# The first part of layer 3 for the last image moved into the loop of the attention layer, with the last chunk convolved in two turns

## The chip, the cores and the metric

The kernel runs on one core of a Trainium2 chip. A core has five engines with queues of their own: TensorE (PE, matrix products), VectorE (DVE), ScalarE (ACT), GpSimd (POOL) and SyncE (SP), which here only issues DMA transfers. An engine takes its instructions in order and waits on semaphores for what others must have finished. On-chip memory is SBUF (128 partitions) and PSUM, into which TensorE writes; DRAM is reached through DMA queues. The metric is the device time of one execution in microseconds. Three runs of the kernel before took 3888.66, 3891.05 and 3893.82 us: the median is 3891.05.

## The reference

A batch of four images of 64 x 64 pixels with 128 channels goes through four layers, one after the other. Layer 0 is neighbourhood attention, layer 1 full attention over the 4096 pixels of an image, layer 2 a gated product with a sum over a row and a layer norm. The change is about layer 3, a selective scan in four directions:

```python
xz = x @ Win                                   # 128 -> 2 x 256
xb, z = jnp.split(xz, 2, axis=-1)
xb = depthwise_conv3x3(xb)                     # 256 channels
xb = jax.nn.silu(xb + conv_b)                  # "u"
xf = xb.reshape(Bb, Cd, L); xt = transposed(xb).reshape(Bb, Cd, L)
xs = jnp.stack([xf, xf[..., ::-1], xt, xt[..., ::-1]], axis=1)
xs_flat = xs.reshape(Bb * K, Cd, L)
x_dbl = jnp.einsum('bcl,cd->bdl', xs_flat, Wxproj)
dt, Bs, Cs = x_dbl[:, :r], x_dbl[:, r:r + N], x_dbl[:, r + N:]     # r = 8, N = 1
dt_kb = dt.reshape(K, Bb, r, L)                # the reshape mixes batch and direction
u_kb = xs_flat.reshape(K, Bb, Cd, L)           # delta, B and C likewise
# scan over L: h = exp(softplus(dt @ Wdt + b) * A) * h + delta * u * B;  y = h * C + u * D
y = (y0 + y1 + y2 + y3).transpose(0, 2, 1)     # directions turned back
yz = y * jax.nn.silu(z)
out = layer_norm(yz) @ Wout
```

The reshape `(Bb * K)` to `(K, Bb)` gives "direction" k of the scan the four stacked sequences of image k, so each image must be through the first part of layer 3 (projection, convolution, SiLU, x_dbl) before its quarter of the scan can run.

## The kernel before, in words

`conv_seq` calls `layers_0_to_2` (L109) and then `layer_3` (L919). Every image is cut into 8 chunks of 512 pixels (8 rows).

**`layers_0_to_2`** runs the images one after the other. For image b it runs layer 0, then `layer_1` (L504 to L624), a loop over 34 steps i. A step scores one block of 128 queries against all keys (L581), copies the scores to SBUF (L584), folds a maximum on VectorE (L586 to L593), subtracts and exponentiates (L598 to L608), multiplies by v (L614) and finishes the block (reciprocal L618, residual L619). At the end of each step the loop calls `between(i)`, which lays other work beside the attention:

- one of four parts of layer 2 for chunk n, at i = 6 + 4n + part: mix (o at L671 on VectorE and L672 on POOL), py (L683), norm (L685 to L700), transpose (L248, L704) and a store of the result x to x3_d (x_d in the profile);
- one step of layer 3's first part, the closure `turn(i)` that `front(b)` (L720 to L883) returns.

After the loop `between` is called for four more i, with layer 0 of the next image taken two pieces at a time between them.

**`front(b)`** works on eight chunks during the attention of image b: chunks 4 to 7 of image b-1, then 0 to 3 of image b, each taking four steps, r = 0 to 3. Steps: `load` xc from x3_d; `project` (two matmuls pi into the tile xh, whose rows are shared with the next chunk); `gate` (two matmuls pz at L758, Silu to zf, store); `begin` (the middle tap on ScalarE), `multiply` (four taps as ScalarE products gsum and tp at L785 and L789, which `add_parts` sums on POOL at L796 and L799) and `add_taps` (four taps on VectorE, L805). `activate` (Silu into the one buffer u0, L808) comes at i = 4k + 7 for the k-th chunk, the last one at i = 33; `lower` (L815 to L832) a step later makes du = D*u, the product pd with Wxproj and its copy dq, stores them in du_d and dbl_d, and loads the row of B, spread over 128 partitions, as bb; `times_b` two steps after activate multiplies u by bb on POOL (L837) and stores it in ub_d. Silus are kept in program order on ScalarE; most of the rest the framework's scheduler may place.

Image 3 has no next image. Its chunks 4 to 7 are done at the start of **`layer_3`**, in a block of its own (L1001 to L1130) with other code: it loads weights (mb, cw, cc, pick), loads the tiles x3T of chunks 3 to 7, makes the output weights gw and bw, projects on PE (L1040, L1045), convolves with three taps on PE (L1057) and six on VectorE (L1064), makes u, du, pd (L1080), a product that spreads B over the partitions (pb, L1092) and multiplies on VectorE (L1105). In the same block zs and zt, the sums of D*u over the images in both orders (2 MB each, for f = 0 and 1), are loaded, added on POOL (L1112, with du at L1074) and stored in z_d; C of images 0 to 2 is transposed (`turn_c`, L969 to L971: load 16 KB, one transpose, a copy, store).

**The scan** (L1132 to L1232) has 64 steps, each for a pair of sequences and 1024 elements: pdt (L1169), Softplus de (L1177), inp = de * ub on POOL (L1179), Exp h (L1189), scan on VectorE (L1203), product with C on VectorE (L1219, or L1214 into yo, added to y by an accumulating DMA on POOL's queue, L1215). For the sequences of image k and direction b with b>>1 equal to k>>1, z_d is added to y by such a DMA as well (L1221). ub and cb are double-buffered tiles of 2 MB (ub_0 and ub_1, cb_0 and cb_1), loaded by SP a part ahead. `turn_c` of image 3 comes after step 1. An output stage follows.

Of the kernel before, what the change touches and what calls it, by code (L numbers as in the profile page):

```python
# [29 lines left out]
P = 128  # L30
# [46 lines left out]
def conv_seq(ctx, tc, x, mata, matb, cols, rows, rpb, dtw, convw, sel, out):  # L77
# [12 lines left out]

    ub_d, zf_d = stored("ub_d"), stored("zf_d")
    du_d = [[dram.tile([P, L], F32, name=f"du_d{i}_{f}") for f in range(2)] for i in range(2)]
    dbl_d = [dram.tile([NDBL, L], F32, name=f"dbl_d{b}") for b in range(B)]
    fronts = x3_d, ub_d, zf_d, du_d, dbl_d
# [9 lines left out]

    layers_0_to_2(tc, xf, mata, matb, rows, rpb, convw, ident, cl, dram, *fronts)
    layer_3(tc, of, matb, dtw, convw, sel, ident, cl, dram, *fronts)


@with_exitstack  # L109
def layers_0_to_2(ctx, tc, xf, mata, matb, rows, rpb, convw, ident, cl, dram, x3_d, ub_d, zf_d, du_d, dbl_d):  # L110
# [605 lines left out]

    def by_image_rows(t):
        return t.rearrange("p (i j) -> p i j", j=W)

    def front(b):  # L720
# [3 lines left out]
        u = wp.tile([P, 2, CH], F32, name="u0", tag="bm1")  # L724
        x_of, parts_of, sums = {}, [], {}
# [5 lines left out]
        def project(i, n):  # L731
# [5 lines left out]
            if n == 4:  # L737
                nc.gpsimd.tensor_copy(xh[:, me, :, 0, :], kept_row)
            elif n > 0:
                nc.gpsimd.tensor_copy(xh[:, me, :, 0, :], xh[:, 1 - me, :, RC, :])  # L740
                nc.gpsimd.tensor_copy(xh[:, 1 - me, :, RC + 1, :], xh[:, me, :, 1, :])
# [11 lines left out]

        def gate(i, n):
            x = x_of.pop((i, n))
            for f in range(2):
# [4 lines left out]
                tc.keep_in_program_order(nc.scalar.activation(zf, pz, AF.Silu))  # L761
# [12 lines left out]
        def taps(n):  # L774

            v = (1, 0) if n < NCH - 1 else (-1, 0)
            return [v, (-1, 1), (1, -1), (1, 1)], [(-v[0], 0), (0, -1), (0, 1), (-1, -1)]

        def multiply(n, f, which):
            for k in which:  # L780
                dy, dx = taps(n)[0][k]
# [4 lines left out]
                else:  # L786
# [3 lines left out]
                    parts_of.append((n, f, k, p))  # L790

        def add_parts():
            for n, f, k, p in parts_of:
                r0, r1, c0, c1 = region(n, *taps(n)[0][k])
                a = by_image_rows(sums[n, f])[:, r0:r1, c0:c1]
                nc.gpsimd.tensor_tensor(a, a, p, ALU.add)  # L796
                if k == 3:
                    acc = accs[n & 1][:, f, :]
                    nc.gpsimd.tensor_tensor(acc, acc, sums.pop((n, f)), ALU.add)  # L799
            parts_of.clear()  # L800

        def add_taps(n, f):
            for dy, dx in taps(n)[1]:
# [3 lines left out]
        def activate(n):  # L807
            tc.keep_in_program_order(nc.scalar.activation(u, accs[n & 1], AF.Silu))  # L808

        def lower(i, n):  # L810

            lo, hi = CH * n, CH * n + CH
            for f in range(2):
                du = tmp.tile([P, CH], F32, name="du", tag="c512", bufs=9)
                nc.scalar.activation(du[:, ::-1] if i & 1 else du, u[:, f, :], AF.Copy, scale=cl("d", 2 * i + f))  # L815
# [5 lines left out]
            for f in range(2):  # L821
                for g in range(4):
                    nc.tensor.matmul(
                        pd[HD * g:HD * g + HD, :], lhsT=wx[:, f, :], rhs=u[:, f, bass.ts(g, P)],
# [4 lines left out]
            for g in range(4):  # L829
                nc.sync.dma_start(dbl_d[i][:, lo + P * g:lo + P * g + P], dq[HD * g:HD * g + NDBL, :])  # L830
            bb = x_of[i, n, "b"] = tmp.tile([P, CH], F32, name="bb0", tag="c512", bufs=9)
            nc.sync.dma_start(bb, dbl_d[i][RANK:RANK + 1, lo:hi][0].partition_broadcast(P))  # L832

        def times_b(i, n):
            bb = x_of.pop((i, n, "b"))
            for f in range(2):
                nc.gpsimd.tensor_tensor(u[:, f, :], u[:, f, :], bb, ALU.mult)  # L837
                nc.sync.dma_start(ub_d[i][f][:, bass.ts(n, CH)], u[:, f, :])
# [5 lines left out]
        takes += [[(b, j)] for j in range(4)] + [[]]  # L844

        def turn(i):
# [8 lines left out]
            if j < 8:  # L855
                if r == 0:
                    for c in takes[j]:
                        project(*c)
                    if j == 7:
                        project_row(b, 4)  # L860
                if now:
                    if r in (0, 2):
                        begin(now[1], r // 2)
                    multiply(now[1], r // 2, ((0, 1), (2, 3))[r & 1])
                    if r in (1, 3):
                        add_taps(now[1], r // 2)
# [6 lines left out]
            for k, c in enumerate(whole):  # L873
                at = 4 * k + 7 if k < 7 else 33
                if c:
                    if i == at:
                        activate(c[1])
                    if i == at + 1:
                        lower(*c)
                    if i == at + 2:  # L880
                        times_b(*c)
# [7 lines left out]
    for b in range(B):  # L889
# [25 lines left out]
        for i in range(NT + 2, NT + 6):  # L915
# [7 lines left out]
def layer_3(ctx, tc, of, matb, dtw, convw, sel, ident, cl, dram, x3_d, ub_d, zf_d, du_d, dbl_d):  # L923
    nc = tc.nc
    def pool(name, bufs=1, **kw):
# [11 lines left out]
    bc_d = [  # L937
        [dbl_d[b][RANK:RANK + 1, :], dbl_d[b][RANK + 1:RANK + 2, :], dram.tile([1, L], F32, name=f"ct_d{b}")]
        for b in range(B)
    ]  # L940

    mb = wp.tile([P, NMB], F32, name="mb")
    nc.sync.dma_start(mb, matb)
    win, wout, wx = (MB[k][0] for k in ("win", "wout", "wx"))

    dbl = wp.tile([P, L], F32, name="dbl")
    done = CH * 4
# [6 lines left out]


# [3 lines left out]
    nc.vector.memset(eps, 1e-5)  # L959
    def by_rows(t):  # L960
        return t.rearrange("p (i j) -> p i j", j=W)

    pick = wp.tile([P, 2, P], F32, name="pick")
    nc.sync.dma_start(pick, sel)

    cts = [wp.tile([W, 2, W], F32, name="ct")] * B

    def turn_c(b, pt):
        nc.tensor.transpose(pt, cts[b][:, 0, :], ident[0:W, 0:W])  # L969
        nc.scalar.copy(cts[b][:, 1, :], pt)  # L970
        nc.sync.dma_start(by_rows(bc_d[b][2])[0], cts[b][:, 1, :])  # L971
# [23 lines left out]

    taps_pe = [(0, 0), (0, -1), (0, 1)]
    taps_ve = [(-1, 0), (-1, -1), (-1, 1), (1, 0), (1, -1), (1, 1)]
    with pool("u", 8) as up, pool("z") as zp, pool("a", 2) as ap, pool("psB", 2, space=PSUM) as psp:  # L1000


        zs = [zp.tile([P, L], F32, name=f"zs{f}") for f in range(2)]
        cw = ap.tile([P, 3, DI], F32, name="cw", tag="cw", bufs=1)
        nc.sync.dma_start(cw, convw[3:6].partition_broadcast(P))
        nc.vector.tensor_tensor(cw, cw, mb[:, win:win + DI].unsqueeze(1).to_broadcast([P, 3, DI]), ALU.mult)
        cc = ap.tile([P, 2, 9], F32, name="cc", tag="cc", bufs=1)
        for f in range(2):
            nc.scalar.dma_start(cc[:, f, :], convw[:, P * f:P * f + P].rearrange("t p -> p t"))
        x3s = {}  # L1010
        for n in range(3, NCH):
            x3s[n] = ap.tile([P, RC, W], F32, name="x3T", tag="x3T", bufs=NCH - 3)
            nc.sync.dma_start(x3s[n], by_rows(x3_d[B - 1][:, bass.ts(n, CH)]))
        for f in range(2):
            nc.vector.tensor_scalar(
                gw[:, f, :], mb[:, wout + C * f:wout + C * f + C], cl("gamma", f), None, ALU.mult
            )
        pb = psp.tile([P, C], F32, name="pb", tag="d")
        for f in range(2):
            bb = ap.tile([P, P], F32, name="bb", tag="bb", bufs=1)  # L1020
            nc.vector.tensor_copy(bb, cl("beta", f).to_broadcast([P, P]))
            nc.tensor.matmul(pb, lhsT=bb, rhs=mb[:, wout + C * f:wout + C * f + C], start=(f == 0), stop=(f == 1))
        nc.vector.tensor_copy(bw, pb)
        share = ap.tile([P, P], F32, name="share", tag="bb", bufs=1)
        nc.vector.memset(share, 1.0 / DI)
# [423 lines left out]
```

## Time and profile before

| quantity | value |
|---|---|
| time of the profiled execution | 3889.84 us |
| its span in the profile | 3888.1 us |
| median of three runs | 3891.05 us |
| PE busy | 3405.7 us (88%) |
| DVE busy | 2775.9 us (71%) |
| ACT busy | 2692.5 us (69%) |
| POOL busy | 1438.4 us (37%) |
| last L618 of images 0, 1, 2, 3 starts at | 780.88, 1555.92, 2336.46, 3114.44 us |
| first pdt of the scan (L1169) starts at | 3227.86 us |

The span is the time from the first to the last record of the profile; some 1.7 us of the execution lie outside it. The profile cuts the span into 40 slices and gives for each the busy share of the engines in tenths. Windows give the same for any stretch, in us. The chain of waits goes back from the last instruction to what released it, again and again: each of its rows has a start, a length, an engine, and a tile or a line. A duration of an instruction is that of its line in the profile. DMA shares are the mean of 16 engines.

### The profile page before, as it was taken

How to read it: one execution, taken by the hardware profiler on the slowest of the kernel's cores; microseconds unless marked ns; L12 is line 12 of the kernel's file. 1: busy time of each engine (PE TensorE's matmuls, PEld its weight loads, DVE VectorE, ACT ScalarE, POOL GpSimd, SP SyncE). 2: the span in 40 equal slices, each digit the busy share in tenths (PEclk: the TensorE clock that was granted, in tenths of full speed). 3: DMA queues.
4: the chain of work that ended last, by engine and by line, in shares of the span. 5: the costliest groups of instructions: out<-in, count | busy, mean ns of one | idle time of the engine just before them, and what ended most of it. 6: DMA issues, size and time to landing. Idle time of an engine off the chain costs nothing.

```text
span 3888.1 us, 68949 instructions
## 1 busy us (share of the span) xinstructions
PE 3405.7 (88%) x26660; PEld 2788.6 (72%) x26660; DVE 2775.9 (71%) x4854; ACT 2692.5 (69%) x4364; POOL 1438.4 (37%) x1535
## 2 busy tenths in 40 slices
PE   6999999989999999899999998999999956665647
PEld 3679999956799998567999995679999822222236
DVE  3657777746677877467778774667787746998978
ACT  3865676767677766686777676767776737998944
POOL 5500022144122222451222214512222245897866
PEclk8999999999999999899999998999999975555569
DMA  5100000131010112310111012100011166998998
GB/s 138 46 1 27 12 13 29 48 95 34 17 48 31 37 31 50 92 35 17 47 28 40 31 48 95 34 17 26 28 37 34 29 228 188 278 272 255 260 280 288
DMA packets 192529, 325.07 MB, mean 84 GB/s; under 512 B 24257, under 2 KB 112190, under 8 KB 185246
## 3 DMA queue, kind: packets, MB, share of 16 engines
q1 hardware_dynamic: 150568, 251.75, 18.6%
q0 software_dynamic: 18624, 58.07, 8.1%
q10 hardware_dynamic: 23008, 10.84, 1.0%
q8 instruction: 210, 3.44, 0.4%
q14 instruction: 119, 0.97, 0.1%
HBM read 179.00 MB, written 108.11 MB: 74 GB/s over the span
## 4 chain that ended last, share of the span: by engine, by line
PE 52%; DVE 18%; ACT 12%; issue 7%; DMA 6%; POOL 4%; SPq 1%; POOLq 0%; ACTq 0%; DVEq 0%
PE po L614 16%; PE sc L581 16%; DVE mx L593 4%; PE pt L465 3%; DVE mx L588 2%; POOL inp L1179 2%; PE sc L430 2%; PE po L476 2%; DMA y<-yo 2%; ACT pr L448 2%; ACT st L584 2%; DVE h L1203 2%; ACT st L608 2%; DVE acc L805 1%; PE pz L758 1%
## 5 line engine op out<-in xcount | busy, mean ns | idle before, releaser
L614 PE MATMUL po<-v,st 128*128 128x129 f32 x8192 | 1087.5, 275 | 4.1 <-ACT st L608 4.1
L581 PE MATMUL sc<-qT,kT 128*128 128x128 f32 x8192 | 1083.2, 276 | 0.4 <-ACT st L584 0.4
L581 PEld LDWEIGHTS sc<-qT,kT 128*128 128x128 f32 x8192 | 1004.0, 193 | 21.8 <-issue 19.0
L614 PEld LDWEIGHTS po<-v,st 128*128 128x128 f32 x8192 | 1002.9, 192 | 7.5 <-issue 6.7
L584 ACT COPY st<-sc 128x512 f32<-128x512 f32 x1024 | 578.0, 584 | 523.9 <-PE sc L581 517.5
L607 DVE TENSOR_TENSOR st<-st,pb 128x2048 f32<-128x2048 f32 x256 | 574.0, 2284 | 49.5 <-PE pb L604 49.4
L588 DVE TENSOR_TENSOR mx<-mx,st 128x1024 f32<-128x1024 f32 x256 | 314.0, 1227 | 251.3 <-ACT st L584 249.1
L608 ACT ACTIVATE st<-st 128x2048 f32<-128x2048 f32 x256 | 482.7, 1908 | 6.6 <-DVE st L607 5.5
L1169 PE MATMUL pdt<-dbl,dt 8*128 8x512 f32 x512 | 307.8, 1088 | 171.6 <-ACT de L1177 170.2
L1179 POOL TENSOR_TENSOR inp<-de,ub 128x1024 f32<-128x1024 f32 x128 | 356.4, 2944 | 74.9 <-ACT de L1177 72.9
L1169 PEld LDWEIGHTS pdt<-dbl,dt 8*128 8x128 f32 x512 | 114.2, 314 | 363.8 <-ACT de L1177 299.6
L456 POOL TENSOR_SCALAR pr<-pr,sm 128x308 f32<-128x308 f32 (+3 forms) x512 | 243.5, 494 | 260.1 <-DVE sm L454 193.2
L676 POOL TENSOR_TENSOR x<-x,row 128x512 f32<-128x512 f32 x32 | 52.2, 1630 | 701.1 <-PE pt L248 701.1
L796 POOL TENSOR_TENSOR gsum<-gsum,tp 128x504 f32<-128x504 f32 (+1 forms) x168 | 231.9, 1380 | 157.9 <-ACT gsum L785 92.4
L448 ACT ACTIVATE pr<-pr,mx 128x308 f32<-128x308 f32 (+3 forms) x512 | 262.5, 517 | 0.0
L593 DVE TENSOR_TENSOR mx<-mx 128x512 f32<-128x512 f32 (+2 forms) x384 | 245.2, 639 | 6.1
L1203 DVE TENSOR_TENSOR_SCAN h<-h,end,inp 128x1024 f32<-128x1024 f32 x96 | 220.7, 2344 | 7.8 <-ACT h L1189 5.5
L465 PE MATMUL pt<-ident,pr 128*88 128x128 f32 (+5 forms) x1472 | 204.4, 276 | 7.9 <-ACT prT L467 7.8
L434 DVE CUSTOM_DVE_ANT_0 pr<-sc,bias_m 128x266 f32<-128x266 f32 (+1 forms) x384 | 151.7, 451 | 70.6 <-PE sc L430 64.8
L465 PEld LDWEIGHTS pt<-ident,pr 128*88 128x88 f32 (+5 forms) x1472 | 163.6, 138 | 45.7 <-ACT prT L467 31.6
L467 ACT COPY prT<-pt 110x512 f32<-110x512 f32 (+3 forms) x240 | 139.1, 579 | 75.6 <-PE pt L465 72.2
L586 DVE TENSOR_TENSOR mx<-st 128x1024 f32<-128x1024 f32 x128 | 169.3, 1323 | 14.4 <-ACT st L584 14.2
(240 smaller groups left out, 5259.7 us busy)
## 6 DMA issues: line engine op xcount, KB each, us to landing
y<-yo POOLq DMA_DIRECT2D x64, 512.0 KB, 12.7
ub_d<-u SPq DMA_DIRECT2D x64, 256.0 KB
ub<-ub_d SPq DMA_DIRECT2D x16, 1024.0 KB
cb<-dbl_d SPq DMA_DIRECT2D x8, 2048.0 KB
cb<-ct_d SPq DMA_DIRECT2D x8, 2048.0 KB
y<-z_d POOLq DMA_DIRECT2D x32, 512.0 KB, 8.1
yn_d<-y SPq DMA_DIRECT2D x32, 512.0 KB
yl<-yn_d SPq DMA_DIRECT2D x64, 256.0 KB
```

The costliest lines, as they stand in the source:

```text
L448: pin(nc.scalar.activation(k.pr[:, h], k.pr[:, h], AF.Exp, bias=k.mx[:, h:h + 1], accum_out=k.sm[:, h:h + 1]))
L465: pin(nc.tensor.transpose(pt[0:n, h, :], k.pr[:, h, at:at + n], ident))
L581: nc.tensor.matmul(ps[:, r, :], lhsT=kT[:, bass.ts(G * g + r, P)], rhs=qT[:, bass.ts(i, P)], start=True, stop=True)
L584: nc.scalar.copy(k.st[:, G * g:G * g + G, :], ps)
L588: nc.vector.tensor_tensor(k.mx, k.mx, k.st[:, 4 * g - 4:4 * g + 4, :], ALU.max)
L593: nc.vector.tensor_tensor(mx[:, 0:n, :], mx[:, 0:n, :], mx[:, n:2 * n, :], ALU.max)
L607: nc.vector.tensor_tensor(part, part, pb.unsqueeze(1).to_broadcast([P, 16, P]), ALU.add)
L608: nc.scalar.activation(part, part, AF.Exp)
L614: nc.tensor.matmul(k.po, lhsT=k.st[:, j, :], rhs=v[:, j, :], start=(j == 0), stop=(j == NT - 1))
L1169: nc.tensor.matmul(pdt[j][:, g, :], lhsT=dt[o:o + RANK, P * f:P * f + P], rhs=at(dbl[o:o + RANK, :], k & 2, g0, g0 + CH), start=True, stop ...
L1179: nc.gpsimd.tensor_tensor(by_rows(inp), by_rows(de), at(ub, b ^ (k & 1), SC * n, SC * n + SC), ALU.mult)
L1203: nc.vector.tensor_tensor_scan(h[:, way], h[:, way], inp[:, way], prev, ALU.mult, ALU.add)
```

## The change

1. `taps`, `multiply`, `add_parts` and `add_taps` know the image. For image 3's chunks 4 to 7 (`at_end`) only two taps go over ScalarE and POOL, and six are VectorE's; their Silus need not keep program order.
2. Chunk 3 (j == 7) of each image is convolved for both halves f in r = 0 and again both in r = 1, two steps earlier than before. `activate` comes at i = 30 for chunk 2 (31 before) and i = 32 for chunk 3 (33 before), and chunk 3's u goes into tiles of its own, u1.
3. For image 3, chunk 4 is loaded, projected (i = 28) and gated (i = 31) in the loop, in place of the one row that was projected before. `end(i)` goes on with chunks 5, 6 and 7 at i = 30, 34 and 38 (load), one later (project and convolve) and two later (gate), and activates and lowers chunks 4 to 7 at i = 34, 37, 41 and 41. B is spread by matmuls from dq, and VectorE multiplies. The loop of `between` goes on to i = 44 for image 3.
4. `turn_c` of image b-1 runs in the attention of image b, at i = 22 and 24; the output weights are made at image 0, i = 3, stored in DRAM as gw_d and bw_d and loaded in `layer_3`.
5. The block of `layer_3` is gone. zs uses the tiles y2 and y3 of the scan, zt the tile ub_1. zs0, zt and zs1 are loaded ahead of the scan; `add_z(0)` and `add_z(1)` run on VectorE after scan steps 2 and 3 and store z_d in quarters; the second zt is loaded between them. ub_1 is loaded half a part later than before. The accumulating DMAs of z_d are collected in `late` and issued two per step after step 3. `turn_c` of image 3 comes after step 5.

```diff
+        def at_end(i, n):
+            return i == B - 1 and n >= 4
...
-        def taps(n):
+        def taps(i, n):
             v = (1, 0) if n < NCH - 1 else (-1, 0)
-            return [v, (-1, 1), (1, -1), (1, 1)], [(-v[0], 0), (0, -1), (0, 1), (-1, -1)]
+            gp, ve = [v, (-1, 1), (1, -1), (1, 1)], [(-v[0], 0), (0, -1), (0, 1), (-1, -1)]
+            return (gp[:2], ve + gp[2:]) if at_end(i, n) else (gp, ve)
...
-        def activate(n):
-            tc.keep_in_program_order(nc.scalar.activation(u, accs[n & 1], AF.Silu))
+        def activate(i, n, apart=False):
+            if apart:
+                u_of[i, n] = [tmp.tile([P, CH], F32, name="u1", tag="c512", bufs=9) for _ in range(2)]
+                for f in range(2):
+                    silu(i, n, u_of[i, n][f], accs[n & 1][:, f, :])
+            else:
+                u_of[i, n] = [u0[:, f, :] for f in range(2)]
+                silu(i, n, u0, accs[n & 1])
...
+            if at_end(i, n):
+                pb = ps_s([P, CH], "pb3")
+                for g in range(4):
+                    r = HD * g + RANK
+                    nc.tensor.matmul(
+                        pb[:, bass.ts(g, P)], lhsT=ident[:, r:r + 1].to_broadcast([P, P]), rhs=dq, start=True, stop=True
+                    )
+                times_b(i, n, pb, nc.vector)
+                return
...
-        takes += [[(b, j)] for j in range(4)] + [[]]
+        takes += [[(b, j)] for j in range(4)] + [[(b, 4)] if b == B - 1 else []]
+        u_at = [4 * k + 7 for k in range(6)] + [30, 32]
+        def convolve(i, n, fs, half):
+            for f in fs:
+                if half == 0:
+                    begin(n, f)
+                multiply(i, n, f, range(len(taps(i, n)[0]))[2 * half:2 * half + 2])
+            for f in fs if half else []:
+                add_taps(i, n, f)
+        def end(i):
+            c = B - 1
+            for n, at in ((5, 30), (6, 34), (7, 38)):
+                if i == at:
+                    load(c, n)
+                if i == at + 1:
+                    project(c, n)
+                    for k in (n - 1, n)[0:1 + (n == NCH - 1)]:
+                        convolve(c, k, range(2), 0)
+                        convolve(c, k, range(2), 1)
+                if i == at + 2:
+                    gate(c, n)
+            for n, at in ((4, 34), (5, 37), (6, 41), (7, 41)):
+                if i == at:
+                    activate(c, n, True)
+                    lower(c, n)
...
-                if now:
-                    if r in (0, 2):
-                        begin(now[1], r // 2)
-                    multiply(now[1], r // 2, ((0, 1), (2, 3))[r & 1])
-                    if r in (1, 3):
-                        add_taps(now[1], r // 2)
+                if now and j < 7:
+                    convolve(*now, (r // 2,), r & 1)
+                elif now and r < 2:
+                    convolve(*now, range(2), r)
...
+            if b > 0 and i in (22, 24):
+                turn_c(b - 1, (i - 22) // 2)
+            if b == 0 and i == 3:
+                output_weights()
+            if b == B - 1:
+                end(i)
...
-        for i in range(NT + 2, NT + 6):
+        for i in range(NT + 2, NT + 6 if b + 1 < B else NT + 11):
```

In `layer_3` the block from `pool("u", 8)` to the stores of z_d (L1001 to L1130) is removed, and these lines are new:

```diff
+    for b in range(B):
+        nc.sync.dma_start(dbl[32 * b:32 * b + NDBL, :], dbl_d[b])
+        if b == 1:
+            load_ub(ub_s[0], 0, 0)
+            load_c(cb_s[0], 0, 0)
...
+    zs, zt = ys[2:4], ub_s[1]
+    def load_z(f, part):
+        nc.sync.dma_start(zt if part else zs[f], du_d[part][f])
+    def add_z(f):
+        nc.vector.tensor_tensor(turned(zs[f]), turned(zs[f]), by_rows(zt), ALU.add)
+        for g in range(4):
+            quarter = bass.ts(g, L // 4)
+            nc.sync.dma_start(z_d[f][:, quarter], zs[f][:, quarter])
+    for f, part in ((0, 0), (0, 1), (1, 0)):
+        load_z(f, part)
+    nc.sync.dma_start(gw, gw_d)
+    nc.sync.dma_start(bw, bw_d)
+    nc.sync.dma_start(ct[:, 0, :], by_rows(bc_d[B - 1][1])[0])
...
-                if half == 0 and j + 1 < len(fks):
+                if half == (j == 0) and j + 1 < len(fks):
                     loads.append((load_ub, ub_s[(j + 1) % 2], *fks[j + 1]))
...
-                    nc.gpsimd.dma_start(y, z_d[f][:, lo:hi], accum_op=ALU.add)
+                    late.append((y, z_d[f][:, lo:hi]))
...
-            if j == 1:
+            for _ in range(2 if j > 3 else 0):
+                if late:
+                    y, z = late.pop(0)
+                    nc.gpsimd.dma_start(y, z, accum_op=ALU.add)
+            if j == 2:
+                add_z(0)
+                load_z(1, 1)
+            if j == 3:
+                add_z(1)
+            if j == 5:
                 turn_c(B - 1, psp.tile([P, 2, CH], F32, name="pt3", tag="dt0", bufs=1)[0:W, 0, 0:W])
```

## The prediction

> **What bounds the kernel now.** I read the slices of the page first, then windows of 20 us between the last attention matmul and the scan, then the chain of waits there and at an image's end.
>
> ```profile
> PE   6999999989999999899999998999999956665647
> POOL 5500022144122222451222214512222245897866
> PEclk8999999999999999899999998999999975555569
> DMA  5100000131010112310111012100011166998998
> ```
>
> A slice is 97.2 us. Up to slice 32 TensorE is full: layers 0 to 2 are bound by it, with dips at the ends of images. From slice 33 its clock is half and DMA is high: the scan, which VectorE bounds (its windows of 28 us from 3284 show 27.57 busy of 28; a step of two scans takes 7.03). Between them lies a hole:
>
> ```profile
> core 0: us, PE busy (x) PEld busy (x) DVE busy (x) ACT busy (x) POOL busy (x), PEclk, DMA share, GB/s
> 3100.00:3120.00 20.00, 17.48 (x149) 15.36 (x148) 10.93 (x24) 8.34 (x8) 5.04 (x5) 1.00 0.35 80
> 3120.00:3140.00 20.00, 4.04 (x28) 2.88 (x28) 4.52 (x16) 7.84 (x11) 5.26 (x5) 0.54 0.43 87
> 3140.00:3160.00 20.00, 8.95 (x16) 4.34 (x17) 2.97 (x12) 1.83 (x4) 0.00 (x0) 0.52 0.94 344
> 3200.00:3220.00 20.00, 5.00 (x19) 1.21 (x20) 1.44 (x3) 4.31 (x10) 3.22 (x2) 0.50 0.52 214
> ```
>
> The last value matmul (L614) ends at 3114.4, the first of the scan (L1169) starts at 3227.86: 113.5 us in which mostly no engine is full. Its chain:
>
> ```profile
> 3114.27 2.50 POOL u L837 x2
> 3116.79 2.10 DMA ub_d<-u
> 3118.97 1.28 ACT L808
> ...
> 3142.57 11.19 DMA x3T<-x_d
> ...
> 3203.69 5.75 DMA ct<-dbl_d
> ...
> 3210.67 3.81 DMA ct<-dbl_d
> ...
> 3219.12 7.31 PE pb L1092 x8
> ```
>
> Three parts: the end of image 3's layers 0 to 2 (to 3142), the other code for its chunks 4 to 7 behind 4 MB of zs and zt (to 3203), then two turns of C in series, pd and pb (to 3227.8). Each image's end has the first part too; image 2's:
>
> ```profile
> 2336.79 2.47 POOL u L837 x2
> 2339.27 2.07 DMA ub_d<-u
> 2341.39 1.28 ACT L808
> ...
> 2347.32 3.90 DMA dbl_d<-dq
> ```
>
> Chunk 3's Silu waits until chunk 2's u, in the one buffer u0, has been stored.
>
> **The change, part by part.**
>
> *Ends of images 0 to 2.* Chunk 3 is convolved two steps earlier and gets its own u1, so the wait for u0 goes and Silu is done before the last L614 ends, at T. Before (T = 2336.42): Silu ends at +7.3, bb lands at +18.2, POOL multiplies and then does o (L672), which ends at +20.8 and releases py. After: pd 0.6, dq 0.6, four store issues 1.4, dbl_d 3.9, bb 3.3 and the gaps put bb near +11.5; POOL 2.5 and o 1.1 give +15. Late next is the same bb. Gain 5.5, taken as 5, three times: **-15**. Bounds -20 (o goes ahead of u on POOL's queue) and 0: in steps 28 to 31 one step gets 8 taps (0.74 each) on VectorE, while another loses them; these three steps take 22.0, 15.2 and 18.4 to 20.0 now and I make them 22.5, 18 and 16.5, level.
>
> *Image 3's attention.* Chunk 4's project and gate (two matmuls of 0.43 to 0.59 and one ACT pass of 0.6 each) and chunk 5's project enter steps 28 to 31; three pairs x 1.9 on the full PE are 5.7. Chunk 4's 12 taps on VectorE, 9 us, lie in step 31 beside 14.3 us of matmuls. **+6**, bounds +3 (PE has spare between) to +12 (taps between maximum and softmax cost what they last).
>
> *After it.* The built order, with the trace's durations, from T: bb +10, POOL u and o +14.6, py +16.7, four taps and x +18.8, norm and transpose +25, x_d stored +30, xc loaded +32.4, pi +34.5, ten ACT passes +40.4, 16 taps of 0.74 (some hidden) +46.5, POOL's gsum and acc (1.38 and 1.41) +50.7, Silu, du, dq +53, pb on PE +54, u on VectorE +55.3, dbl_d stored and dbl loaded +59.5, where L1169 can start. du_d's sums stay on POOL's queue, 8 issues of 1.0, beside it. gw, C's turns, mb, cw and pick are out of it: the turns (0.3 PE, 0.2 ACT) lie in full steps 22 and 24 of the next image, at nothing; uncovered each would be 10 us as here.
> One place is not sure. In SP's built order the 2 MB of zs stand ahead of the last x_d store and of xc's load, and zs1 and C's 2 MB ahead of the last dbl_d stores. The row: x3T, 256 KB behind such loads, took 11.19. The Trainium skill, "DMA: Bandwidth & Descriptors", section "Anatomy of one DMA", has 2.0 us plus bytes / 436e3, measured for transfers issued by GpSimd: 2.6 us for 256 KB, which agrees with bb's 3.06 to 3.31 here on an idle queue. By the page the tail is 59.5, by the row 68; zs alone is half of what stood before x3T, and it starts some us earlier, so I take 2.5 more: 62, bounds 55 (taps hidden whole) and 80 (both waits, and POOL's sums queued behind others). Against 113.5: **-51.5**, bounds -58.5 to -33.5.
>
> *In the scan.* VectorE adds zs and zt twice (128x4096, by columns), where POOL did it for 11.83 each in the hole. Nearest row: L607, 2048 elements in 2.28, so 4.6 each, 9.2, all on the bound. But "SBUF — State Buffer", section "SBUF: two separate sides", says that a VectorE instruction with two SBUF inputs and a GpSimd instruction exclude each other for their whole length. That speaks against this part: POOL's inp (L1179, 2.33 to 3.68 in the first ten steps, median 2.66) fills the scan. A trace of it: in 3042 to 3048, beside POOL's sums, a fold of L593 took 1.81, the line's median being 0.43. By the rule each add waits up to one inp, 2 x (4.6 + 2.9) = 15; by the row 9.2. I take half a wait: **+12**, bounds 9 and 18 (slower by columns).
> DMA: zt twice, z_d twice, zs1, ub and cb at the start, and ub_1 that may load only when zt is free: 8.4 to 11 MB, 24 to 33 us at some 340 GB/s. The first four windows of the scan have shares of 0.66, 0.76, 0.57 and 1.03, so 28 us free. I take **+4** for ub_1 late at k=1; bounds 0 and +16 (POOL's inp waits behind the delayed y<-z_d sums on its queue, and the inp after those).
>
> *Output weights* at image 0, step 3: six small matmuls that may wait for wo's load on PE's queue: **+1**, 0 to 3.
>
> Sum: -15 + 6 - 51.5 + 12 + 4 + 1 = **-43.5**. The profiled execution took 3889.84 (span 3888.1 and 1.7 around it), so 3846.3; the median of the runs is 1.2 above it: 3847.5, say **3847**.
>
> **Rivals.**
> - *Half the gain sinks in the scan*: both DMA and lock at their upper ends, 18 + 16 for 16, and the odd parts' stalls grow. For it: those stalls stand now (13 us from 3509, in which y's store takes 31.6), and DMA shares of 1.03 to 1.05 from 3424. Against it: steps 1 to 3 have slack. 3847 + 18 = 3865. 18%.
> - *Nothing at the image ends*: o stays behind u on POOL and the 8 taps delay the maximum. For it: PE is full there, and steps 28 to 31 hold both. 3847 + 15 = 3862. 15%.
> - *Tail by its lower end, or an early o*: taps lie beside ACT and nothing waits for zs. -7 and -5, and add at 9: 3847 - 15 = 3832; with all at the low ends 3822. 20%.
> - *Slower*: one mechanism, in the scan: the eight delayed y<-z_d sums of the first parts. They sit on POOL's queue between inp and inp; if each must wait there until z_d or its y is ready, and takes its 8.1 us to land before the next, POOL gives 65 us away and VectorE follows, since it waits for inp. For it: VectorE adds z only after step 2, and the sums share the queue with y<-yo, which takes 12.7. Against it: the same sums run now in steps 0 to 3 and the steps stay at 7.03. Price -43.5 - 4 + 65 = +17.5: 3909. It decides from some 60 us given back in the scan. 3%.
> - *It does nothing*: the scheduler sets image 3's chunks 6 and 7 serially behind each other with nothing hidden, at half clock, so that the tail is as long as the old 113.5 less little: 3889. 3%.
>
> **Numbers.** Forecast 41%: 3847, between 3835 and 3856. The range takes in the rivals on both sides up to the doubtful sums: 3818 to 3870, leaving out the two last cases and the very ends of the others. What measurement can tell from no change is about 0.2%, 7.8 us. Faster by more: 0.94; within: 0.03; slower by more: 0.03.
>
> **What would show it.** Image ends: the last L618 of an image to the next image's first, 257.7 to 262.9 now, shorter by 5, and no wait of Silu for ub_d. The stretch from the last L614 to the first L1169: 62 instead of 113.5, with x_d to xc the longest transfer; if near 70, the row of x3T was right. The adds: two VectorE rows of 4.6 us with 128x4096; if 7 or more, columns or the lock cost. In the windows of the scan's first 56 us VectorE is as full as now if the DMA hides; a wait of POOL's inp for ub at k=1 is the sign that it doesn't. Wrong would be above all: a scan that is over 30 us longer, or image ends no shorter.

## The result, and the profile after

The changed kernel takes 3860.61 us (median of 4 runs, 3853.97 to 3861.60) against 3891.11 (4 runs, 3888.66 to 3893.82); the ratio is 0.9918, with a 95% interval of 0.9901 to 0.9935. It is faster by 0.8%, 30 us; the forecast was 3847, within 3818 to 3870. The profiled execution took 3861.60 with a span of 3859.8, 28.3 us shorter than the 3888.1 of before.

The slices, tenths of busy time in 40 equal parts of 96.5 us:

```profile
PE   6999999999999999999999999999999944665647
POOL 5510022244122222441223224412222346888866
PEclk7999999999999999999999999999999955555579
DMA  5100000121010112210111022100011176998998
```

The dips of PE at the ends of images no longer show in the row, and the hole before the scan is still there in slices 32 and 33. Cutting the span at five events gives the sum. The events are the first and the last reciprocal of an image's attention (L618, now L623) and the first product of the scan (L1169, now L1144), each by its start:

| stretch | before | after | difference | foreseen |
|---|---|---|---|---|
| start to the first L623 | 275.96 | 276.19 | +0.2 | +1 (output weights) |
| attention of images 0 to 2, sum | 1539.92 | 1528.04 | -11.9 | 0 |
| ends of images 0 to 2 to the next first L623, sum | 780.35 | 763.10 | -17.3 | -15 |
| attention of image 3 | 518.21 | 518.97 | +0.8 | +6 |
| last L623 to the first L1144 ("tail") | 113.42 | 81.34 | -32.1 | -51.5 |
| the first L1144 to the end ("scan") | 660.24 | 692.16 | +31.9 | +16 |

The sum of the differences is the 28.3 us. Its last two rows cancel: what the change is mostly made of, the removal of layer 3's block, has moved 32 us from ahead of the scan into it.

The tail, in windows of 20 us (busy us of each engine, with the count of instructions):

```profile
core 0: us, PE busy (x) PEld busy (x) DVE busy (x) ACT busy (x) POOL busy (x), PEclk, DMA share, GB/s
3100.00:3120.00 20.00, 9.75 (x45) 5.25 (x44) 14.76 (x28) 13.57 (x20) 10.15 (x10) 0.76 0.39 96
3120.00:3140.00 20.00, 7.46 (x12) 3.05 (x11) 5.00 (x7) 5.41 (x9) 2.00 (x2) 0.54 0.99 345
3140.00:3160.00 20.00, 6.76 (x48) 4.36 (x48) 15.35 (x16) 9.87 (x17) 14.83 (x12) 0.55 0.54 132
3160.00:3180.00 20.00, 12.36 (x20) 5.79 (x22) 0.94 (x3) 5.43 (x6) 7.00 (x4) 0.50 1.07 300
```

From 3120 to 3140 the engines mostly stand (PE is busy for 7.46 us of 20, VectorE for 5.00), while the DMA engines are full (share 0.99). The chain of waits (start, length, who) says on what, and goes on into the scan:

```profile
3118.23 11.13 DMA x_d<-x
...
3129.42 2.89 DMA xc<-x_d
...
3137.71 13.79 DVE acc L822 x12
...
3159.38 8.25 issue
3167.64 10.29 PE pdt L1144 x16
...
3229.58 10.51 DVE y L1106
...
3241.03 14.67 DMA z_d<-y
```

x_d's store is 256 KB and takes 11.13 us: 0.85 us before it SP issued the 2 MB of zs. Then come the taps of chunks 6 and 7, then 8.25 us that the chain can only call "issue": before the first pdt, PE needs dbl, whose first load SP issued at 3161.3. That it is this load is read from `z_late` and `best2` below. In the scan one addition of zs and zt (tile y, L1106) takes 10.5, and VectorE waits for the store of z_d. VectorE's own timeline there (start, length, line, and in brackets the idle time before it and its cause):

```profile
3202.58 10.85 DVE L1106 TENSOR_TENSOR y<-y,ub 128x4096 f32<-128x4096 f32 x1
...
3229.49 10.60 DVE L1106 TENSOR_TENSOR y<-y,ub 128x4096 f32<-128x4096 f32 x1
...
3255.72 2.47 DVE L1194 TENSOR_TENSOR y<-h,cb 128x1024 f32<-128x1024 f32 x2 [10.65 <-DMA z_d<-y]
```

10.85 + 10.60 + 10.65 = 32.1 us: as much as the scan has grown by. The third term comes from the tiles: zs lies in y2 and y3, so the first y of images 2 and 3 may be written only when z_d's store has read the old content.

At an image's end (image 2) the chain now reads

```profile
2312.42 0.18 DVE ri L623
...
2315.96 4.27 DMA dbl_d<-dq
2320.23 0.02 issue
2320.25 3.24 DMA bb<-dbl_d
...
2326.10 1.02 POOL o L677
```

No Silu and no store of u stand ahead of dbl_d's store, and o ends 14.7 us after the last value product (L619, L614 before) is through at 2312.40; before it was 20.8.

### The profile page after: what moved, and what is told of

The parts are those of the page before. It is cut to its first block, busy times and chain, and to the rows that moved or that the text cites. A ratio compares the mean times of both kernels' runs of the same rounds, so it can differ in the third digit from the quotient of the medians.

```text
span 3859.8 us, 69106 instructions
## 1 busy us (share of the span) xinstructions
PE 3378.9 (88%) x26676; PEld 2778.6 (72%) x26676; DVE 2806.5 (73%) x4855; ACT 2705.7 (70%) x4391; POOL 1443.5 (37%) x1556
## 4 chain that ended last, share of the span: by engine, by line
PE 52%; DVE 20%; ACT 11%; issue 7%; DMA 6%; POOL 4%; SPq 1%; DVEq 0%; POOLq 0%; ACTq 0%
PE po L619 16%; PE sc L586 16%; DVE mx L598 4%; PE pt L470 3%; DVE mx L593 2%; POOL inp L1154 2%; PE sc L435 2%; PE po L481 2%; DVE acc L822 2%; DMA y<-yo 2%; DVE h L1178 2%; ACT pr L453 2%; ACT st L589 2%; ACT st L613 1%; PE pz L772 1%
## 5 line engine op out<-in xcount | busy, mean ns | idle before, releaser
L619 PE MATMUL po<-v,st 128*128 128x129 f32 x8192 | 1084.0, 275 | 4.1 <-ACT st L613 4.1
L619 PEld LDWEIGHTS po<-v,st 128*128 128x128 f32 x8192 | 999.0, 192 | 5.8 <-issue 5.8
L1144 PE MATMUL pdt<-dbl,dt 8*128 8x512 f32 x512 | 308.5, 1088 | 194.6 <-ACT de L1152 186.4
L1144 PEld LDWEIGHTS pdt<-dbl,dt 8*128 8x128 f32 x512 | 115.8, 314 | 384.6 <-ACT de L1152 314.4
L813 POOL TENSOR_TENSOR gsum<-gsum,tp 128x504 f32<-128x504 f32 (+1 forms) x176 | 246.0, 1399 | 152.5 <-ACT gsum L801 83.4
L822 DVE SCALAR_TENSOR_TENSOR acc<-xh,cc,acc 128x504 f32<-128x504 f32 (+3 forms) x272 | 217.3, 832 | 17.8 <-ACT acc L786 16.9
```

The lines of the kernel that those rows point to most:

```text
L619: nc.tensor.matmul(k.po, lhsT=k.st[:, j, :], rhs=v[:, j, :], start=(j == 0), stop=(j == NT - 1))
L1144: nc.tensor.matmul(pdt[j][:, g, :], lhsT=dt[o:o + RANK, P * f:P * f + P], rhs=at(dbl[o:o + RANK, :], k & 2, g0, g0 + CH), start=True, stop ...
```

## The experiments

All times are to be held against the kernel before on the same chip, whose median was 3885.78 for `undo_ends`, `own_u_only`, `turns_only` and `add_forms`, 3887.23 for `no_add`, `no_z`, `z_late` and `add_early`, 3892.53 for `ends_only`, `best1` and `best2`; so ratios are given. The stretches are of the profiled executions. Stretches with the same code differ between kernels: the three image ends of the six kernels that share the changed kernel's code there lie between 756.7 and 763.1 in sum, so differences of less than 7 are not read in the ends. The attention of the same six agrees within 1.0 (images 0 to 2) and 0.7 (image 3).

**Chunk 3's course, undone and taken apart.** Three kernels change only the image ends of the changed kernel.

`undo_ends` puts all of it back:

```diff
-        u_at = [4 * k + 7 for k in range(6)] + [30, 32]
+        u_at = [4 * k + 7 for k in range(7)] + [33]
...
-                if now and j < 7:
+                if now:
                     convolve(*now, (r // 2,), r & 1)
-                elif now and r < 2:
-                    convolve(*now, range(2), r)
...
-                    activate(*c, at == 32)
+                    activate(*c)
```

> The changed kernel with chunk 3's old course: convolved over four steps, activated at 33 into u0 (chunk 2 at 31). Theory: the image ends give 17 us and the attention of images 0 to 2 another 12 through this part, so the stretches from an image's last L618 to the next first one go back to 257 to 263 us, images 0 to 2 take 12 us more together, and the time is near 3889. Rival (the attention got shorter through something else, such as C's turns or the schedule as a whole): only the ends go back, 3878.

Measured: 3890.0, ratio 1.0009 (1.0000 to 1.0017). Attention of images 0 to 2 1539.4, ends 778.1, image 3 523.9, tail 81.2, scan 693.0. The theory holds. And with the ends undone nothing is left: the removal of layer 3's block, with all the code that runs image 3's chunks inside the loop, is worth nothing as it was built. Image 3's attention is 5.6 us longer than before the change, the 6 that the prediction put there; in the changed kernel it is 519.0.

`own_u_only` is the same with the last line kept as `activate(*c, at == 33)`, so that chunk 3 keeps its buffer u1.

> As undo_ends, but chunk 3's u keeps its own buffer u1. Theory: u0 alone is what the image ends wait for, so these stay at 254 to 255 us and only the 12 us of the attention come back: 3872. Rival (Silu at 33 is late in any case, since the convolution ends only in step 31): ends at 257 or more, 3880 to 3889.

Measured: 3874.35, ratio 0.9972 (0.9961 to 0.9983); ends 766.5, attention of images 0 to 2 1540.1. As the theory said: the buffer alone frees the ends, and gives nothing to the attention of images 0 to 2. Image 3's attention is 519.9 here, so the buffer alone takes back 4 of the 5.6 us too.

`turns_only` keeps the two turns and the earlier times, and lets chunk 3 share u0:

```diff
-                    activate(*c, at == 32)
+                    activate(*c)
```

> The changed kernel with chunk 3's u in u0, all else as changed (two turns, Silu at 32). Theory: ScalarE, whose Silus keep program order, stands in step 32 until chunk 2's u is multiplied and stored (2.5 + 2.1 us) and the attention behind it waits: steps 28 to 33 grow by 3 to 5 us an image, 3870 to 3880. Rival (the wait now lies under the attention, and the two turns alone do the whole): 3861 within 4.

Measured: 3851.41, ratio 0.9909 (0.9895 to 0.9924); ends 757.6, attention 1528.0. The rival is right: the buffer is not needed once chunk 2 is a step earlier. ScalarE's timeline around image 2's last softmax shows why no wait is left:

```profile
2299.32 3.71 ACT L613 ACTIVATE st<-st 128x2048 f32<-128x2048 f32 x2
2303.05 1.28 ACT L697 ACT_TABLE_LOAD   x1
2304.34 0.30 ACT L697 ACTIVATE rd<-mv,eps 128x4 f32<-128x4 f32 x1
2304.82 1.28 ACT L764 ACT_TABLE_LOAD   x1 [0.18 <-DMA ub_d<-u]
2306.11 1.06 ACT L764 ACTIVATE u<-acc 128x1024 f32<-128x1024 f32 x1
```

The Silu comes after the last exponentials, waits 0.18 us for u0, and has run before the attention ends at 2308.8.

So two ways remove the wait, and the turns give the attention's 12 us besides. The seven intervals between the last eight finished blocks of image 2 show where: 17.0, 17.6, 21.8, 15.0, 20.0, 8.9, 8.8 before; 17.0, 17.6, 20.0, 15.6, 15.8, 9.6, 8.0 after, and the same with turns_only to 0.1; 17.0, 17.6, 23.8, 15.3, 18.4, 8.9, 8.8 with own_u_only. In images 0 and 1 the third was 22.7 and 22.0 and the fifth 18.4 in both; after the change they are 20.0 and 20.5, and 15.8. Over the three images the third interval falls by 5.9 us, the fifth by 9.3, and the rest give 3.3 back.

In the fifth the chain of before (image 2) goes through three folds of the maximum, while POOL sums the parts of chunk 3's second half:

```profile
2301.09 0.84 DVE mx L593
2301.95 1.38 DVE mx L593
2303.35 1.23 DVE mx L593
```

```profile
2299.18 2.19 POOL L676 TENSOR_TENSOR x<-x,row 128x512 f32<-128x512 f32 x1 [23.84 <-PE pt L248]
2301.32 4.44 POOL L796 TENSOR_TENSOR gsum<-gsum,tp 128x504 f32<-128x504 f32 x3
```

With the two turns these sums are done two intervals earlier, and the same folds in the chain of after read

```profile
2279.13 1.60 DVE mx L598
...
2281.59 0.34 DVE mx L598
2281.95 0.30 DVE mx L598
```

The first stands beside an addition of POOL's, the other two beside none:

```profile
2278.59 1.59 POOL L681 TENSOR_TENSOR x<-x,row 128x512 f32<-128x512 f32 x1 [16.59 <-PE pt L253]
```

In the third interval a fold and a tap stand beside POOL's sums in the chain of before, and for the most part in a gap between two sums in that of after:

```profile
2267.12 1.28 DVE mx L593
...
2268.49 1.56 DVE acc L805
```

```profile
2248.43 0.41 DVE mx L598
...
2248.93 0.63 DVE acc L822
```

All of these read SBUF twice, as the additions below do, and their lengths fit that. Added up, the folds and taps of the third interval are shorter by 1.8, 1.4 and 1.8 us in images 0, 1 and 2, those of the fifth by 1.2 in each: 8.5 of the 15.2 us that the two intervals lose in sum. The rest was not tried by itself, and why the fifth took 20.0 in image 2 with the same rows as at 18.4 stays open.

**This part alone.** `ends_only` takes the kernel before and gives it the two turns and the earlier times, nothing else:

```diff
-                if now:
-                    if r in (0, 2):
-                        begin(now[1], r // 2)
-                    multiply(now[1], r // 2, ((0, 1), (2, 3))[r & 1])
-                    if r in (1, 3):
-                        add_taps(now[1], r // 2)
+                for f in range(2) if now and j == 7 and r < 2 else [r // 2] if now and j < 7 else []:
+                    half = r if j == 7 else r & 1
+                    if half == 0:
+                        begin(now[1], f)
+                    multiply(now[1], f, ((0, 1), (2, 3))[half])
+                    if half == 1:
+                        add_taps(now[1], f)
...
-                at = 4 * k + 7 if k < 7 else 33
+                at = 4 * k + 7 if k < 6 else (30, 32)[k - 6]
```

> The kernel before, with nothing of the change but chunk 3's course: convolved in two turns, activated at 32 (chunk 2 at 30), one buffer u0. Layer 3 keeps its block ahead of the scan. Theory: this small part is the whole gain and the rest nets to nothing: three image ends 6 to 9 us shorter each, the attention of images 0 to 2 by 12 together, image 3's by 3 to 5, the scan at 660: 3845 to 3856. Rival (the rest of the change brings a good part, and this alone is worth the 17 us of the ends): 3870 to 3880.

Measured: 3852.70, ratio 0.9900 (0.9885 to 0.9914). Ends 760.6, attention of images 0 to 2 1526.6, image 3 514.7, tail 106.6, scan 666.5. These lines give what the whole change gives. The tail and the scan are 773.1 together, 773.7 before: the tail is shorter by 6.8 and the scan longer by 6.3, and that is not explained here.

**Where the scan's 32 us lie.** `no_add` leaves out the two additions; z_d is stored from zs alone:

```diff
-        nc.vector.tensor_tensor(turned(zs[f]), turned(zs[f]), by_rows(zt), ALU.add)
```

> The changed kernel without the two additions of zs and zt on VectorE; the loads, the stores of z_d (from zs alone) and their sums into y stay. The scan (first L1144 to the end) took 692.2 us, before the change 660.2. Theory: the additions cost their own length, 2 x 10.7, and the wait of y for z_d's stores another 10.6 that stays: the scan takes 671, the time falls by 21. Rival (the wait hangs on the second addition coming late, so both go): 660, by 32.

Measured: 3826.57, ratio 0.9838 (0.9822 to 0.9854), scan 663.8. The rival is nearly right (it had 660): VectorE waits for no store of z_d in this trace, so the 10.65 us go with the additions. The second addition is what makes the second store late; `add_early` below, which has it sooner, has no such wait either.

`no_z` leaves out the loads of zs and zt, the additions and z_d's stores, and sums du_d's first half into y:

```diff
-                    late.append((y, z_d[f][:, lo:hi]))
+                    late.append((y, du_d[0][f][:, lo:hi]))
...
-    for f, part in ((0, 0), (0, 1), (1, 0)):
-        load_z(f, part)
...
-            if j == 2:
-                add_z(0)
-                load_z(1, 1)
-            if j == 3:
-                add_z(1)
```

> The changed kernel without loads of zs and zt, additions and stores of z_d; du_d's first half is summed into y in z_d's place, so only the second half's addend is left out. Theory: z is all that the scan gained, so it takes 660, as before the change. Rival (ub_1 loaded half a part late, the delayed sums on POOL's queue or C's late turn cost something too): 665 or more.

Measured: 3820.75, ratio 0.9827 (0.9812 to 0.9841); scan 658.9, before the change 660.2. z is the whole; ub_1's later load and the delayed sums cost nothing that shows. The tail is 74.9 here: zs no longer stands before x_d, whose store takes 5.12.

**Why an addition takes 10.7.** `add_forms` has f = 0 with only zt by columns, f = 1 with none (the second sum is then of unturned data):

```diff
-        nc.vector.tensor_tensor(turned(zs[f]), turned(zs[f]), by_rows(zt), ALU.add)
+        nc.vector.tensor_tensor(by_rows(zs[f]), by_rows(zs[f]), by_rows(zt) if f else turned(zt), ALU.add)
```

> The two additions of zs and zt in other forms: f = 0 with zs by rows and only zt read by columns (the same sum), f = 1 with both by rows (the second sum is then not turned; only its time is looked at). Now both take 10.7 us. Theory (columns cost: two operands with a step of 64 elements): f = 0 falls to 6 to 8, f = 1 to 4.6, the time by 9 to 15: 3846 to 3852. Rival (the lock between VectorE and POOL's inp is the cost): both stay at 8 to 10.7, 3856 to 3861.

Measured: 3849.86, ratio 0.9907 (0.9892 to 0.9922); the additions 9.43 and 6.35, both above what the theory had (6 to 8 and 4.6), and the second below the rival's 8. Both are at work. VectorE and POOL of this kernel, from their timelines:

```profile
3192.62 9.43 DVE L1106 TENSOR_TENSOR y<-y,ub 128x4096 f32<-128x4096 f32 x1
...
3218.19 6.35 DVE L1106 TENSOR_TENSOR y<-y,ub 128x4096 f32<-128x4096 f32 x1
```

```profile
3189.33 5.68 POOL L1154 TENSOR_TENSOR inp<-de,ub 128x1024 f32<-128x1024 f32 x2 [2.43 <-ACT de L1152]
...
3215.87 4.38 POOL L1154 TENSOR_TENSOR inp<-de,ub 128x1024 f32<-128x1024 f32 x1
...
3222.38 4.88 POOL L1154 TENSOR_TENSOR inp<-de,ub 128x1024 f32<-128x1024 f32 x1
```

The first addition starts at 3192.62 and POOL's products end at 3195.01, 2.39 later; the second at 3218.19, with POOL's product ending at 3220.25, 2.06 later. Taken off, 7.04 and 4.29 us are left, and 4.29 for 4096 elements is a little under twice L607's 2.28 for 2048 before. Then the inp that starts at 3222.38 ends at 3227.26, 2.7 us after the addition's end at 3224.54, where an undisturbed one takes 2.33. The changed kernel tells the same: its POOL rows

```profile
3199.29 5.67 POOL L1154 TENSOR_TENSOR inp<-de,ub 128x1024 f32<-128x1024 f32 x2 [2.44 <-ACT de L1152]
...
3227.16 4.40 POOL L1154 TENSOR_TENSOR inp<-de,ub 128x1024 f32<-128x1024 f32 x1
...
3233.68 9.03 POOL L1154 TENSOR_TENSOR inp<-de,ub 128x1024 f32<-128x1024 f32 x1
```

end 2.38 and 2.07 us into the two additions, which leaves 8.47 and 8.53 for them. Two additions of later runs had no product of POOL's running when they began, the first of `add_early` (one operand by columns) and the second of `z_late` (one tile read and written by columns):

```profile
3182.77 7.18 DVE L1109 TENSOR_TENSOR y<-y,ub 128x4096 f32<-128x4096 f32 x1 [1.73 <-DMA ub<-du_d]
```

```profile
3217.51 8.91 DVE L1107 TENSOR_TENSOR y<-y,ub 128x4096 f32<-128x4096 f32 x1
```

They took 7.18 and 8.91 whole. So an addition is 4.3 by rows (seen once), 7.0 to 7.2 with one operand read by columns, 8.5 to 8.9 with one tile read and written by columns, and what a product of POOL's still has to run is added to it; POOL in turn stands until the addition ends. The Trainium skill, "SBUF — State Buffer", section "SBUF: two separate sides", has this exclusion; the numbers are what it costs here.

**Mending.** `z_late` issues the early loads behind that of image 3's last chunk (`last_load` holds the load of xc, and what stands under `issue_after` is issued only after it):

```diff
-    for f, part in ((0, 0), (0, 1), (1, 0)):
-        load_z(f, part)
+    with tc.issue_after(last_load[0]):
+        for f, part in ((0, 0), (0, 1), (1, 0)):
+            load_z(f, part)
...
-            for load, *args in loads:
-                load(*args)
+            with tc.issue_after(last_load[0]):
+                for load, *args in loads:
+                    load(*args)
```

> The changed kernel with the loads of zs, zt and the second C issued behind the load of image 3's last chunk. In the changed kernel x_d's last store took 11.1 us right behind the 2 MB of zs. Theory: it takes 2 to 3.5 now, and the stretch from the last L623 to the first L1144 falls from 81.3 to 73 with nothing lost in the scan: 8 us less. Rival (the transfers are only moved: dbl or cb come later by as much): 79 to 82 in that stretch or a longer scan, 3856 to 3862.

Measured: 3848.63, ratio 0.9897 (0.9882 to 0.9912). The tail is 74.6 instead of 81.3, the scan 689.7. In its chain

```profile
3111.42 4.70 DMA x_d<-x
...
3148.06 6.61 DMA dbl<-dbl_d
```

x_d's store takes 4.70 instead of 11.13, near the 5.12 of `no_z`, which loads no zs: what zs cost there was its place ahead of the store in SP's queue. The theory holds, with a store longer than its 2 to 3.5. The chain also names the load of dbl as the last wait before the scan.

`add_early` puts the additions behind steps 0 and 2, held there, with zs by rows:

```diff
-        nc.vector.tensor_tensor(turned(zs[f]), turned(zs[f]), by_rows(zt), ALU.add)
+        add = tc.keep_in_program_order(
+            nc.vector.tensor_tensor(by_rows(zs[f]), by_rows(zs[f]), turned(zt), ALU.add)
+        )
...
+        behind[:] = [add.ins]
...
-            for step, (_, inp), h in zip(pair, parts, hs):
-                back(*step, inp, h)
+            with tc.issue_after(behind.pop()) if behind else nullcontext():
+                for step, (_, inp), h in zip(pair, parts, hs):
+                    back(*step, inp, h)
...
-            if j == 2:
+            if j == 0:
                 add_z(0)
                 load_z(1, 1)
-            if j == 3:
+            if j == 2:
                 add_z(1)
```

> The changed kernel with the additions after scan steps 0 and 2 (2 and 3, where the second in fact ran behind step 5's first scan), kept there on VectorE's queue, and with zs by rows and zt by columns. Theory: the second store of z_d lands before y is written there, so the wait of 10.6 us goes, and each addition takes 7 to 9.4: the scan falls from 692 to 678, the time by 13 to 15. Rival (zt has not landed after step 0, VectorE waits for it, and the saturated DMA is as late as before): 688 or more.

Measured: 3839.37, ratio 0.9870 (0.9853 to 0.9886); additions 7.18 and 10.32, the second with a product of POOL's that ends 3.26 us into it, which leaves 7.06; scan 682.3. The wait for z_d is gone; the scan is 4 longer than the theory had (678), of which 1.7 is a wait for zt.

`best1` joins add_early, z_late and turns_only.

> The changed kernel with the additions early (as add_early), the loads of zs, zt and the second C behind the last chunk's load (as z_late), and u0 for chunk 3 (as turns_only). Theory: the three gains lie in different stretches and add: tail 73 to 75, scan 680 to 684, image ends 250 to 254: 3828 to 3836. Rival (zs now lands later, and the additions after step 0 wait for zt longer than in add_early): scan 690, 3840.

Measured: 3838.03, ratio 0.9868 (0.9851 to 0.9884); tail 73.8, scan 678.1, image ends 761.0. The stretches come out about as expected, the time 2 us above the theory's range; it can't be told from add_early. By 1.3% against before these two are the fastest of the kernels here that compute the whole. `ends_only`, beside which best1 ran, is 14.7 us slower: so much, 0.4%, is the removal of the block worth once its additions and loads are mended.

`best2` places the tiles of layer 3 in another order, so that dbl of images 0 and 1 can be loaded early, and puts the loads of dbl, ub_0 and cb_0 behind the last chunk's load too:

```diff
+    ub_1 = yp.tile([P, L], F32, name="ub_1")
+    y01 = [yp.tile([P, L], F32, name=f"y{b}") for b in range(2)]
     wp = ctx.enter_context(pool("wb"))
...
+    cb_s.append(zp.tile([P, L], F32, name="cb_1"))
+    ys = y01 + [zp.tile([P, L], F32, name=f"y{b}") for b in range(2, B)]
```

> best1 with the tiles of layer 3 placed otherwise: dbl, ub_0 and cb_0 lie where memory is free at the end of the attention, and dbl of images 0 and 1 is loaded before the last chunk is through, since the scan's first four steps read nothing of image 3. Theory: the first L1155 no longer waits 6 to 8 us for dbl, and starts right after the last pb: tail 66 to 68, 3820 to 3829. Rival (the scan then waits for ub_0 and cb_0, which are issued as late as before): tail 67, but scan 6 to 8 longer, as best1.

Measured: 3844.79, ratio 0.9877 (0.9860 to 0.9893). The tail is 65.2, 8.6 us less than in best1, where the chain waits 6.3 for dbl just before the first product; but the scan is 694.9, 16.8 more, and both theories are too kind to it. zs is now issued only behind the last chunk's stores (at 3157.10, in best1 at 3120.36). VectorE waits 9.8 us for zt before the first addition, 3.0 for cb and 4.2 for z_d's store, 17.0 in sum; best1 has none of the three. zt has landed 98.3 us after the last reciprocal of the attention, in best1 after 94.8 at the latest, so an earlier start of the scan gains nothing.

## Why the prediction was right or wrong

The sign and the range were right, and the 17 us of the image ends nearly as worked out (15); the time lies outside the narrower forecast, 3835 to 3856. Where the gain comes from was forecast wrongly. The removal of the block (image 3's attention, the tail and the scan together) was worked out at -29.5 and came to +0.6; the steps of the attention that were called level gave 11.9. The sum of -43.5 was too large by 15 us, from errors of both signs, and that it lies in the range is partly luck: without the 11.9 that nobody foresaw the time would have been some 3872. By the sign that the prediction itself set for being wrong, a scan that is over 30 us longer, its account of the scan was wrong (31.9).

- *Ends of images 0 to 2* (-15): -17.3, by the mechanism named, o ending at +14.7 where +15 was written. undo_ends, own_u_only and turns_only show the cause, the wait for u0; of the two measures that the prediction joined, either alone removes it.
- *Steps 28 to 31 "level"*: the attention gave 11.9. The prediction looked at VectorE's taps alone, 8 in one step and none in another, and let them cancel. In the traces the taps do not move: six of chunk 3's eight run in the second of the seven intervals above and two in the third, before and after. What moved were POOL's sums, from the fifth interval into the third, away from the folds beside them.
- *Image 3's attention* (+6): right for the work added (undo_ends: +5.6), and hidden again, for the most part by the buffer alone (own_u_only: +1.7).
- *Tail* (62): 81.3. Four terms were too small. x_d's store was issued at +31.9, 6.9 us after the +25 of norm and transpose, which ran mixed with taps. The store took 11.13, where 5 and "I take 2.5 more" give 7.5: the row of x3T, 11.19, was the right one, and the page's sum, which is for one transfer, the wrong one; bb's 3.06 to 3.31 already lay above its 2.6. z_late gives 6.7 us of the tail back. From pi to the last tap there are 19.3 us in place of 12.0: 14 taps stand in the chain with 1.15 each, POOL's sums beside them, where 0.74 was used and some were to be hidden. And dbl took 8.3 where 5.5 had been worked out.
- *Scan, the additions* (+12, up to 18): 21.5. The term that failed is the 4.6 of an addition, taken from a row by rows with one operand in PSUM, for a tile read and written by columns, which takes 8.5; the wait for POOL was taken as 1.5 and is 2.2. add_forms separates them. The prediction named VectorE as the bound; ScalarE is as full in the window that it quotes (27.56 of 28), and the additions cost their full length all the same.
- *Scan, DMA* (+4): 10.65, and not from ub_1. The wait for tiles was not seen: that zs shares y2 and y3 makes the store of z_d a condition for the scan's fifth step. no_add and no_z show that nothing else in the scan costs anything that can be told.
- *Output weights* (+1) and C's turns (0): +0.2 up to the first L623, and nothing later that could be told.

Of the rivals, "nothing at the image ends" (3862) was nearest in number and wrong in substance, since the ends gave 17.3. "Half the gain sinks in the scan" (3865, given 18%) was right in substance: it had 34 us for the scan, which grew by 31.9, though a third of that is the wait for tiles, which it did not name.

## What to carry to other kernels

Cut a span at events that both kernels have and sum the stretches before crediting a change: here the large part moved 32 us from one stretch into another, and a shift of a few lines was the gain. When a block is taken off the path, list what its buffers and loads will stand in front of: a scratch tile that is reused needs its store to land first, and a large load that is ready early is issued ahead of a small one that the chain needs. Work moved onto an engine that bounds a stretch costs its full length there, with its access pattern and its waits for the neighbour engine; price it by a row with the same pattern. When two engines share a stretch, look for rows that are longer than the same rows elsewhere: here that is how the wait for the other engine showed.

## What the runs showed of the hardware

- An addition of 128x4096 on VectorE costs 4.3 us by rows (once, add_forms), 7.0 to 7.2 with one operand by columns (steps of 64 floats; add_forms, add_early) and 8.5 to 8.9 with one tile read and written by columns (the changed kernel, z_late).
- VectorE's additions with two SBUF inputs and POOL's products waited for each other in every case looked at, the later one for the whole rest of the earlier one: 2.06 to 2.39 us on VectorE in add_forms and the changed kernel, 3.26 in add_early, where the product's row starts 0.02 us behind the addition's and still went first, and nothing where no product ran; and an inp of 9.03 us on POOL. The wait shows as a longer row and not as idle time.
- A store of 256 KB issued 0.85 us behind a load of 2 MB took 11.13 us (11.40 in add_early), where 4.70 stood when that load came later and 5.12 without it (no_z).
